# Masking and exponentiating kept attention scores before their transposition, with seven block products in every group

## The chip, the cores and the metric

The kernel runs on one core of one Trainium2 chip, as a single launch. The metric is the device time of that core in microseconds (us); lower is better. A core has five engines that run their own instruction queues in order: TensorE (PE in the profile, with PEld for its weight loads), VectorE (DVE), ScalarE (ACT), GpSimd (POOL) and SyncE (SP), the last two of which mostly issue DMAs here.

## The reference, cut to what matters

Four graph layers on 2708 nodes with 512 features. Only layers 2 and 3 are touched by the change. Layer 2 is a masked softmax whose scores are symmetric before the mask, because queries and keys are the same matrix `h`:

```python
def _L2_gnn_ref(x, adj, weight, bias, node_w, edge_w):
    node_att = softmax(x @ node_w, axis=0)
    h = x @ edge_w
    e = h @ h.T
    e = where(adj > 0, e, -9e15)
    edge_att = softmax(e, axis=1)
    output = adj * (node_att * edge_att) @ (x @ weight)
    return output + bias

def _L3_gnn_ref(x, adj_matrix, spatial_matrix, Wq, bq, ...):
    a = (x @ Wq + bq) @ (x @ Wk + bk).T / sqrt(512)
    a = a + adj_matrix + spatial_matrix        # both are adj
    return softmax(a, axis=-1) @ (x @ Wv + bv)

x = layernorm(x + L2(x, adj));  x = layernorm(x + L3(x, adj, adj))
```

All data is fp32. `adj` itself is not symmetric: `adjT` is a second input with the transposed matrix.

## The kernel before

**Tiles.** The 2708 rows make 22 blocks of 128 (the last has 20 rows) and 11 groups of two blocks. Groups 0 to 9 are full, group 10, the remnant, has 128 + 20 rows. A layer's attention is a walk over pairs (query group gi, key group g): 11 × 11 = 121 steps, the 11 keys of a query group one after the other in the order of `key_order`. A tile of one pair is 128 partitions × 2 × 256: keys on partitions, the group's 256 queries along the row.

**The pipeline of a pair.** `one_score` loads the mask tile with SyncE, forms the scores (sixteen 128x256 matmul records in a full pair, since an fp32 product takes two records) and masks them: ScalarE turns the mask into 0 or −9e15 (L1742), VectorE takes the minimum with the scores out of PSUM into the tile `e` (L1743) and updates a running maximum (L1328). When a group's 11 pairs are scored, `largest` and `spread` make the negated maximum of each query and lay it along the row of every partition (`nmax`). `begin_exp` adds `nmax` (VectorE, L1386) and exponentiates (ScalarE, L1387); `end_exp` adds the tile to the running sum `acc` (VectorE, L1398), loads the mask tile again and multiplies with it (VectorE, L1746), and prepares the differences `T` for the products. `one_sum` multiplies with the values on TensorE (L1444) into the banks `po`, and `end` adds the banks up and queues the group's normalization and projection in `later`. The pair of step t is scored at step t, exponentiated at t − 11 and summed at t − 12 (`LAG = NG + 1`).

**Symmetry.** In layer 2 (`mirror`) the raw scores of a pair with g > gi are copied (`s_raw`) and written to DRAM (`kept`). When the roles turn (g < gi) they are read back with queries on partitions (`s_kept`), transposed by four 128x128 TensorE transposes (L1276) into PSUM, and from there masked as any other pair. There are 55 such turned pairs. In a group's own pair (g = gi) only three of four blocks are computed; the fourth is the transpose of the block that ScalarE copies to `s_own` (L1312, L1314).

**Seven or eight products.** A full pair of 2 × 2 blocks needs eight block products with the value halves, or seven with combined values (`S`, made by `combine`) and the differences `T`, of which VectorE makes four blocks in three operations (L1408). Layer 3 uses seven in every group. Layer 2 uses seven in query groups 0 to 5 and eight from `PLAIN_FROM = 6` on. `combine` overwrites one half of the values, so the original is saved to DRAM (`v2_d`, L1654) and loaded back by GpSimd around group 5 (L1893).

**Order.** A loop over t calls layer 2's step, from step 126 on (`start3 = steps + 5`) layer 3's step, then one item of `later`. The order of instructions on each engine is not the order of the text: the framework's scheduler interleaves them. SyncE's loads stand in one queue; a load waits there until its buffer is free (four mask buffers `a_cols`, two `s_kept`), and what stands behind it waits too.

Of the kernel before, what the change touches and what calls it, by code (L numbers as in the profile page):

```python
# [29 lines left out]
def gnn_stack_kernel(  # L30
# [1157 lines left out]
    v2_d = dram.tile([P, NG - 1, HF], F32, name="v2_d")  # L1188
# [27 lines left out]
    def softmax_layer(  # L1216
        att, psum, later, keys, vals, query, score, weigh, load_rest, finish, mirror, plain_from
# [30 lines left out]
        def load_a(gi, g):  # L1248
            c0, w = GSPAN[gi]
            j0, m = GSPAN[g]  # L1250
            a = att.tile([P, GROUP, GW], F32, tag="a", name="a_cols", bufs=4)
            src = adjT[j0 : j0 + m, c0 : c0 + w]
            if g != REMNANT:
                nc.sync.dma_start(a[:, :, :w], src.rearrange("(b p) i -> p b i", p=P))
                return a
            nc.vector.memset(a[:, 1, :], 0.0)
            nc.sync.dma_start(a[:, 0, :w], src[:P])
            for r in range(0, P, Q):
                nc.sync.dma_start(a[r : r + REST, 1, :w], src[P:])
            return a  # L1260

        def one_score(st, k):
            gi, g = st["gi"], st["order"][k]
            c0, w = GSPAN[gi]
            j0, m = GSPAN[g]
            a = load_a(gi, g)
            ps = psum.tile([P, GROUP, GW], F32, tag="ps_s", name="ps_s")
            e = att.tile([P, GROUP, GW], F32, tag="e", name="e", bufs=LAG + 2)
            sizes = [BLOCKS[it][1] for it in GROUPS[gi]]
            if mirror and g < gi:  # L1270
                s = att.tile([P, GROUP, GW], F32, tag="q", name="s_kept", bufs=2)
                for dst, src in rows_of(gi, s, kept[g, gi]):
                    nc.sync.dma_start(dst, src)
                for jb in range(GROUP):
                    for b, n in enumerate(sizes):
                        nc.tensor.transpose(  # L1276
                            ps[:, jb, b * P : b * P + n],
                            s[:n, b, jb * P : (jb + 1) * P],
                            ident[:n, :n],
                        )  # L1280
            else:
                own = mirror and g == gi
                for jb, jt in enumerate(GROUPS[g]):
                    j = BLOCKS[jt][0]
                    if jt == NT - 1:

                        parts = psum.tile([P, BANK], F32, tag="tp", name="ps_parts")
                        for c in range(C):
                            nc.tensor.matmul(  # L1289
                                parts[c * Q : (c + 1) * Q, :w],  # L1290
                                keys[:, c, j : j + Q],
                                st["q"][:, c, :],
                                start=True,
                                stop=True,
                            )
                        nc.scalar.copy(e[:, 1, :w], parts[:, :w])
                        nc.tensor.matmul(
                            ps[:, 1, :w], quarters, e[:, 1, :w], start=True, stop=True
                        )
                        continue  # L1300
                    i = jb * P if own else 0
                    for c in range(C):
                        nc.tensor.matmul(  # L1303
                            ps[:, jb, i:w],
                            keys[:, c, j : j + P],
                            st["q"][:, c, i:],
                            start=(c == 0),
                            stop=(c == C - 1),
                        )
                    if own and jb == 0 and g != REMNANT:  # L1310
                        s = att.tile([P, GROUP, GW], F32, tag="x", name="s_own", bufs=4)
                        nc.scalar.copy(s[:, 0, :P], ps[:, 0, P:])  # L1312
                    elif own and jb == 1:
                        nc.tensor.transpose(ps[:, 1, :P], s[:, 0, :P], ident)  # L1314
            if mirror and g > gi:
                s = att.tile([P, GROUP, GW], F32, tag="x", name="s_raw", bufs=4)
                nc.scalar.copy(s, ps)
                for dst, src in rows_of(g, s, kept[gi, g]):
                    nc.gpsimd.dma_start(src, dst)
            score(e[:, :, :w], ps[:, :, :w], a[:, :, :w])  # L1320
            st["e"].append(e)
            if k == 1:
                st["mx"] = att.tile([P, GROUP, GW], F32, tag="mx", name="mx", bufs=1)
                nc.vector.tensor_tensor(
                    st["mx"][:, :, :w], st["e"][0][:, :, :w], e[:, :, :w], ALU.max
                )
            elif k > 1:
                in_pairs(g, w, lambda p: nc.vector.tensor_tensor(*p, ALU.max), st["mx"], st["mx"], e)  # L1328

        def in_pairs(g, w, do, *tiles):  # L1330

            if g != REMNANT:
                do([t[:, :, :w] for t in tiles])
            else:
                do([t[:, 0, :w] for t in tiles])
                do([t[:REST, 1, :w] for t in tiles])

        def largest(st):
# [3 lines left out]
            mx = st["mx"]  # L1342
            nc.vector.tensor_tensor(mx[:, 0, :w], mx[:, 0, :w], mx[:, 1, :w], ALU.max)
            tp = psum.tile([P, C, P], F32, tag="tp", name="tp_mx")
            nm = small.tile([P, GROUP], F32, tag="nm", name="nm")
            dg = att.tile([P, GROUP, P], F32, tag="dg", name="dg", bufs=1)
            sizes = [BLOCKS[it][1] for it in GROUPS[gi]]
            for b, n in enumerate(sizes):
                nc.tensor.transpose(tp[:n, b, :], mx[:, 0, b * P : b * P + n], ident)
            runs = [(0, GROUP, P)] if gi != REMNANT else [(b, 1, n) for b, n in enumerate(sizes)]  # L1350
            for b, count, n in runs:
# [4 lines left out]
                nc.vector.tensor_tensor(  # L1356
                    dg[:n, some, :n],
                    ident[:n, :n].unsqueeze(1).to_broadcast([n, count, n]),
                    nm[:n, some].unsqueeze(2).to_broadcast([n, count, n]),
                    ALU.mult,  # L1360
                )
            st["dg"] = dg

        def spread(st):

            gi, dg = st["gi"], st["dg"]
            w = GSPAN[gi][1]
            pb = psum.tile([P, BANK], F32, tag="tp", name="pb")
            if gi != REMNANT:
                nc.tensor.matmul(  # L1370
                    pb[:, :w], ones, dg.rearrange("p b i -> p (b i)"), start=True, stop=True
                )
            else:
                for b, it in enumerate(GROUPS[gi]):
                    n = BLOCKS[it][1]
                    nc.tensor.matmul(
                        pb[:, b * P : b * P + n], ones[:n], dg[:n, b, :n], start=True, stop=True
                    )
            st["nmax"] = att.tile([P, GW], F32, tag="nmax", name="nmax", bufs=2)
            nc.scalar.copy(st["nmax"][:, :w], pb[:, :w])  # L1380

        def begin_exp(st, k):
            w = GSPAN[st["gi"]][1]
            e = st["e"][k][:, :, :w]
            nm = st["nmax"][:, :w].unsqueeze(1).to_broadcast([P, GROUP, w])
            nc.vector.tensor_tensor(e, e, nm, ALU.add)  # L1386
            nc.scalar.activation(e, e, AF.Exp)  # L1387

        def end_exp(st, k):
# [3 lines left out]
            if k == 0:  # L1393
                st["acc"] = att.tile([P, GROUP, GW], F32, tag="acc", name="acc", bufs=1)
                nc.vector.tensor_copy(st["acc"][:, :, :w], e[:, :, :w])
            else:
                acc = st["acc"]
                in_pairs(g, w, lambda p: nc.vector.tensor_tensor(*p, ALU.add), acc, acc, e)  # L1398
            if weigh:
                weigh(e[:, :, :w], load_a(gi, g)[:, :, :w])  # L1400
            if g != REMNANT and gi < plain_from:
# [10 lines left out]
                st.setdefault("t", {})[k] = t  # L1412
# [3 lines left out]
        def row_sums(st):  # L1416
# [4 lines left out]
            nc.vector.tensor_tensor(acc[:, 0, :w], acc[:, 0, :w], acc[:, 1, :w], ALU.add)  # L1421
            pr = psum.tile([P, BANK], F32, tag="tp", name="pr")
            rs = small.tile([P, GROUP], F32, tag="rs", name="rs")
            for b, it in enumerate(GROUPS[gi]):
                n = BLOCKS[it][1]
                nc.tensor.matmul(
# [6 lines left out]
                nc.vector.reciprocal(rs[:n, b : b + 1], pr[:n, b : b + 1])  # L1433
            st["rs"] = rs

        def one_sum(st, k):
# [16 lines left out]
            if gi == REMNANT:  # L1453
                i = [slice(0, P), slice(w - Q, w)]
                if g != REMNANT:
                    v0, v1 = full[:, GROUP * g, :], full[:, GROUP * g + 1, :]
                    terms = [(0, e[:, 0], v0[:, :HF]), (0, e[:, 1], v1[:, :HF])]
                    if gi < plain_from:
                        d = st["t"].pop(k).rearrange("p q i -> p (q i)")
                        terms += [(1, e[:, 0], S[:, g, 0, :]), (1, d, v1[:, HF:])]  # L1460
                    else:
# [517 lines left out]
```

## Time and profile before

| what | value |
|---|---|
| time, median of 3 runs | 3224.51 us (3223.3 to 3234.12) |
| profiled execution, its own time | 3230.21 us |
| its span, first to last instruction | 3228.4 us |
| layer 2's attention, by the trace | from 1617 us to about 2340 us |
| layer 3's attention | from about 2356 us to the end |
| TensorE, VectorE, ScalarE busy over the span | 98%, 66%, 42% |
| granted TensorE clock over the span | 0.995 |

A busy line of the profile gives an engine's busy time and instruction count. A matmul's duration in the trace includes the pipeline's depth and overlaps its neighbours: a 128x256 record has a mean of 386 ns, while records that follow each other without a wait start 216 ns apart. Matmul cost is therefore counted here by the distance between starts, and a wait of TensorE shorter than about 0.15 us cannot be seen in its busy share.

### The profile page before, as it was taken

How to read it: one execution, taken by the hardware profiler on the slowest of the kernel's cores; microseconds unless marked ns; L12 is line 12 of the kernel's file. 1: busy time of each engine (PE TensorE's matmuls, PEld its weight loads, DVE VectorE, ACT ScalarE, POOL GpSimd, SP SyncE). 2: the span in 40 equal slices, each digit the busy share in tenths (PEclk: the TensorE clock that was granted, in tenths of full speed). 3: DMA queues.
4: the chain of work that ended last, by engine and by line, in shares of the span. 5: the costliest groups of instructions: out<-in, count | busy, mean ns of one | idle time of the engine just before them, and what ended most of it. 6: DMA issues, size and time to landing. Idle time of an engine off the chain costs nothing. (4 is left out here: it accounts for less than half of the span.)

```text
span 3228.4 us, 35961 instructions
## 1 busy us (share of the span) xinstructions
PE 3169.6 (98%) x13440; PEld 2144.0 (66%) x13440; DVE 2122.0 (66%) x3654; ACT 1345.5 (42%) x1460; POOL 212.2 (7%) x316
## 2 busy tenths in 40 slices
PE   8999999999999999999999999999999999999999
PEld 5444444444444446875587887777668888888886
DVE  7889987876686685444366677866645555555565
ACT  6898896477867451001133333433311111111111
POOL 1100100000000000001111111211110000000000
PEclk9999999999999999999999999999999999999999
DMA  7867865156455414541154444555441111111110
GB/s 273 309 226 249 291 231 201 45 173 221 172 173 197 156 58 119 143 113 48 54 155 128 134 144 138 169 153 168 121 127 41 49 49 49 49 52 49 49 51 29
DMA packets 209240, 432.42 MB, mean 134 GB/s; under 512 B 22186, under 2 KB 138774, under 8 KB 203242
## 3 DMA queue, kind: packets, MB, share of 16 engines
q1 hardware_dynamic: 184370, 324.15, 32.9%
q0 software_dynamic: 24256, 103.88, 8.8%
q8 instruction: 105, 1.72, 0.2%
q10 hardware_dynamic: 440, 2.10, 0.2%
q14 instruction: 69, 0.57, 0.1%
HBM read 331.38 MB, written 97.21 MB: 133 GB/s over the span
## 5 line engine op out<-in xcount | busy, mean ns | idle before, releaser
L416 DVE SCALAR_TENSOR_TENSOR t<-t,a 128x2708 f32<-128x2708 f32 (+1 forms) x152 | 450.2, 2975 | 144.6 <-ACT t L408 140.5
L1444 PE MATMUL po<-sup,e 128*128 128x256 f32 (+1 forms) x2000 | 497.4, 386 | 8.1 <-DVE e L1746 6.6
L408 ACT ACTIVATE t<-f1b,f2h 128x1354 f32<-128x1354 f32 (+1 forms) x304 | 415.8, 1412 | 46.9 <-PE po L504 36.4
L417 ACT ACTIVATE t<-t 128x2708 f32<-128x2708 f32 (+1 forms) x152 | 373.2, 2456 | 99.7 <-DVE t L416 99.5
L504 PE MATMUL po<-t,xw 128*128 128x452 f32 (+3 forms) x1056 | 410.3, 552 | 4.2 <-ACT t L417 3.6
L1303 PE MATMUL ps_s<-q,hT 128*128 128x256 f32 (+1 forms) x1848 | 405.6, 372 | 0.0
L504 PE MATMUL po<-t,emb 128*128 128x452 f32 (+3 forms) x1056 | 398.9, 546 | 4.0 <-ACT t L417 3.8
L1444 PEld LDWEIGHTS po<-sup,e 128*128 128x128 f32 (+1 forms) x2000 | 348.4, 185 | 77.1 <-issue 22.4
L1303 PEld LDWEIGHTS ps_s<-q,hT 128*128 128x128 f32 x1848 | 340.0, 190 | 50.4 <-issue 6.7
L504 PEld LDWEIGHTS po<-t,xw 128*128 128x128 f32 (+1 forms) x1056 | 189.6, 190 | 213.2 <-issue 196.1
L504 PEld LDWEIGHTS po<-t,emb 128*128 128x128 f32 (+1 forms) x1056 | 194.0, 191 | 202.0 <-issue 191.7
L1832 DVE SCALAR_TENSOR_TENSOR e<-a_cols,ps_s 128x512 f32<-128x512 f32 (+1 forms) x121 | 80.2, 663 | 284.8 <-PE ps_s L1303 249.5
L1444 PE MATMUL po<-held,T 128*128 128x256 f32 x960 | 240.2, 384 | 0.9 <-DVE T L1408 0.8
L1303 PE MATMUL ps_s<-hT 128*128 128x256 f32 (+2 forms) x968 | 215.8, 373 | 8.1 <-ACT s_own L1312 7.5
L1387 ACT ACTIVATE e<-e 128x512 f32<-128x512 f32 (+1 forms) x242 | 143.4, 612 | 147.0 <-DVE e L1386 146.3
L1303 PEld LDWEIGHTS ps_s<-hT 128*128 128x128 f32 x968 | 178.3, 192 | 38.0 <-ACT s_own L1312 10.7
L1742 ACT ACTIVATE a_cols<-a_cols,neg_big 128x512 f32<-128x512 f32 (+1 forms) x121 | 85.1, 704 | 278.5 <-DMA a_cols<-in_adjT_dram 228.3
L1444 PEld LDWEIGHTS po<-held,T 128*128 128x128 f32 x960 | 182.3, 192 | 28.1 <-DVE T L1408 2.7
L1156 PE MATMUL ps_nb<-hid_hi,at 128*128 128x512 f32 x484 | 185.6, 390 | 0.4 <-DVE at L1148 0.4
L1156 PE MATMUL ps_nb<-hid_lo,at 128*128 128x512 f32 x462 | 180.1, 390 | 0.0
L1386 DVE TENSOR_TENSOR e<-e,nmax 128x512 f32<-128x512 f32 (+1 forms) x242 | 154.6, 666 | 18.0 <-ACT nmax L1380 16.8
L1824 ACT ACTIVATE q<-ps_wide,uq 128x256 f32<-128x256 f32 (+1 forms) x44 | 20.5, 466 | 326.7 <-PE ps_wide L1207 326.7
(267 smaller groups left out, 3906.1 us busy)
## 6 DMA issues: line engine op xcount, KB each, us to landing
a_cols<-in_adjT_dram SPq DMA_DIRECT2D x300, 256.0 KB
a<-adj_d SPq DMA_DIRECT2D x108, 677.0 KB
a<-in_adjT_dram SPq DMA_DIRECT2D x42, 677.0 KB
adj_d<-a POOLq DMA_DIRECT2D x42, 677.0 KB, 5.1
kept<-t POOLq DMA_DIRECT2D x20, 1354.0 KB, 6.6
t<-kept SPq DMA_DIRECT2D x20, 1354.0 KB
raw<-in_adjT_dram SPq DMA_DIRECT2D x105, 256.0 KB
scores<-s_raw POOLq DMA_DIRECT2D x45, 256.0 KB, 3.0
```

The lines of the kernel that those rows point to most:

```text
L408: tanh = nc.scalar.activation(tv[:, k, :], f1b[k][:n, :w], AF.Tanh, bias=f2h[:n, jt, h : h + 1], scale=0.5,)
L416: step = nc.vector.scalar_tensor_tensor(tv, tv, GUARD, ab, ALU.add, ALU.mult)
L417: exp = nc.scalar.activation(tv, tv, AF.Exp, scale=0.5)
L504: nc.tensor.matmul(po[HB * k + q][:, :qw], values[r : r + n, jt, h * P : (h + 1) * P], t[r : r + n, k, q0 : q0 + qw], start=(place == 0), ...
L1156: nc.tensor.matmul(pos[it][:n], at, half[:, jt, :], start=(jt == 0 and k == 0), stop=(jt == NT - 1),)
L1303: nc.tensor.matmul(ps[:, jb, i:w], keys[:, c, j : j + P], st["q"][:, c, i:], start=(c == 0), stop=(c == C - 1),)
L1386: nc.vector.tensor_tensor(e, e, nm, ALU.add)
L1387: nc.scalar.activation(e, e, AF.Exp)
L1444: nc.tensor.matmul(po[bank][rows, half, :], lhsT, rhs, start=(k == 0 and half == 0) if first is None else first, stop=last, skip_group_che ...
L1742: nc.scalar.activation(a, a, AF.Identity, bias=neg_big[: a.shape[0]], scale=1.0e30)
L1824: lambda o, ps: nc.scalar.activation(q[:, o, :w], ps, AF.Identity, bias=uq[:, o : o + 1]),
L1832: nc.vector.scalar_tensor_tensor(e, a, 2.0, ps, ALU.mult, ALU.add)
```

## The change

In layer 2 a turned pair is no longer transposed before it is masked. The kept scores are loaded straight into the tile `e`, with queries on partitions, beside a tile of `adj` itself (not `adjT`); masking and running maximum take place in that layout (`score_rows`). The maximum of the turned pairs is a reduction along the row (`largest`). `begin_exp` exponentiates with the maximum as ScalarE's per-partition bias, one instruction for each of the two blocks, and takes the row sums with the same instructions (`accum_out`); the addition of `nmax` and the addition to `acc` fall away for these pairs. In `end_exp` four transposes bring the exponentiated tile to PSUM, and the multiplication with the mask reads it from there. `row_sums` adds the two kinds of sums.

Every group of both layers now uses seven products; `PLAIN_FROM`, `v2_d` and its loads are gone. Score masks have buffers of their own in layer 2 (three `a_score`), the four `a_cols` hold the weights alone, and each load is put into the program a step before its use (`fetch`, `fetch_weights`). `begin_exp` stands a step further ahead of the sum: `LAG = NG + 2`, `start3 = steps + 6`, `e` has `lag + 3` buffers. In own and remnant pairs the part that waits for a ScalarE copy (`rest`) stands behind the step's products. `spread` uses the maximum as a broadcast weight against the identity instead of a diagonal matrix.

```diff
@@ begin_exp, end_exp
         def begin_exp(st, k):
-            w = GSPAN[st["gi"]][1]
-            e = st["e"][k][:, :, :w]
-            nm = st["nmax"][:, :w].unsqueeze(1).to_broadcast([P, GROUP, w])
-            nc.vector.tensor_tensor(e, e, nm, ALU.add)
-            nc.scalar.activation(e, e, AF.Exp)
+            gi, g = st["gi"], st["order"][k]
+            w = GSPAN[gi][1]
+            if not turned(gi, g):
+                e = st["e"][k][:, :, :w]
+                nm = st["nmax"][:, :w].unsqueeze(1).to_broadcast([P, GROUP, w])
+                nc.vector.tensor_tensor(e, e, nm, ALU.add)
+                nc.scalar.activation(e, e, AF.Exp)
+                return
+            m = st["count"][0]
+            st["count"][0] += 1
...
+            for b, it in enumerate(GROUPS[gi]):
+                n = BLOCKS[it][1]
+                e = st["e"][k][:n, b, :]
+                nc.scalar.activation(
+                    e, e, AF.Exp, bias=st["nm"][:n, b : b + 1],
+                    accum_out=st["sums"][:n, b, m : m + 1],
+                )
...
+            if turned(gi, g):
+                ps = psum.tile([P, GROUP, GW], F32, tag="ps_s", name="ps_e")
+                for jb in range(GROUP):
+                    for b, it in enumerate(GROUPS[gi]):
+                        n = BLOCKS[it][1]
+                        nc.tensor.transpose(
+                            ps[:, jb, b * P : b * P + n],
+                            e[:n, b, jb * P : (jb + 1) * P],
+                            ident[:n, :n],
+                        )
+                weigh(e[:, :, :w], ps[:, :, :w], st["wa"].pop(k)[:, :, :w])
...
-            if g != REMNANT and gi < plain_from:
+            if g != REMNANT:
                 t = att.tile([P, 2 * GROUP, P], F32, tag="T", name="T", bufs=2)
@@ new: fetch, fetch_weights, score_rows
+        def fetch(t):
...
+            e = att.tile([P, GROUP, GW], F32, tag="e", name="e", bufs=lag + 3)
+            st["e"].append(e)
+            a = tile_a()
+            st["a"].append(a)
+            if not turned(gi, g):
+                load_a(a, gi, g)
+                return
+            i0, w = GSPAN[gi]
+            j0 = GSPAN[g][0]
+            for dst, src in rows_of(gi, a, adj[i0 : i0 + w, j0 : j0 + GW]):
+                nc.sync.dma_start(dst, src)
+            for dst, src in rows_of(gi, e, kept[g, gi]):
+                nc.sync.dma_start(dst, src)
+        def fetch_weights(t):
+            gi, k = divmod(t, NG)
+            a = att.tile([P, GROUP, GW], F32, tag="a", name="a_cols", bufs=4)
+            states[gi]["wa"][k] = load_a(a, gi, states[gi]["order"][k])
+        def score_rows(st, k):
+            gi, e, a = st["gi"], st["e"][k], st["a"][k]
+            for x, y in by_rows(gi, e, a):
+                score(x, x, y)
+            running_max(st, k, "rows")
@@ one_sum
-            if gi >= plain_from:
-                for jb, jt in enumerate(GROUPS[g]):
-                    if jt != NT - 1:
-                        for b, i in enumerate((i1, i2)):
-                            for h in range(2):
-                                product(
-                                    2 * b + h,
...
@@ the step
+            if 0 <= t + AHEAD < total:
+                fetch(t + AHEAD)
+            if weigh and 0 <= t + AHEAD + 1 - lag < total:
+                fetch_weights(t + AHEAD + 1 - lag)
+            front = t + 2 - lag
...
@@ the main loop
-    LAG = NG + 1
-    PLAIN_FROM = 6
+    AHEAD = 1
+    LAG = NG + 2
...
-        start3 = steps + 5
+        start3 = steps + 6
```

## The prediction, made before the changed kernel was run

> **What bounds the kernel now.** I read the page's busy shares first, then the stretches of layer 2 one group at a time (from one group's maximum to the next), then TensorE's waits there, then the chain of waits for the cost of one product.
>
> ```profile
> PE 3169.6 (98%) x13440; PEld 2144.0 (66%) x13440; DVE 2122.0 (66%) x3654; ACT 1345.5 (42%) x1460; POOL 212.2 (7%) x316
> ```
>
> TensorE is the bound of the whole. The stretches, with length, busy time by engine, TensorE's clock, DMA share and GB/s:
>
> ```profile
> core 0: us, PE busy (x) PEld busy (x) DVE busy (x) ACT busy (x) POOL busy (x), PEclk, DMA share, GB/s
> 2003.20:2069.20 66.00, 63.33 (x296) 50.02 (x295) 52.37 (x115) 24.19 (x39) 12.84 (x19) 0.97 0.56 163
> 2069.20:2139.20 70.00, 65.43 (x303) 52.46 (x301) 44.00 (x84) 24.98 (x40) 9.40 (x12) 0.95 0.50 148
> 2139.20:2201.00 61.80, 59.43 (x293) 47.98 (x292) 41.44 (x78) 21.16 (x35) 8.97 (x9) 1.00 0.54 159
> 2201.00:2262.10 61.10, 58.59 (x281) 46.39 (x280) 41.77 (x79) 22.71 (x36) 12.03 (x8) 0.97 0.58 172
> 2262.10:2322.90 60.80, 57.60 (x268) 43.44 (x267) 37.03 (x80) 19.08 (x32) 5.71 (x6) 1.00 0.42 116
> 2577.60:2655.90 78.30, 78.30 (x376) 67.83 (x375) 43.75 (x101) 12.67 (x22) 1.08 (x2) 1.00 0.18 50
> ```
>
> The last row is a group of layer 3: no visible idle time. The four before it sum groups 6 to 9, those with eight products. Counting each matmul record by the distance at which its kind follows itself (216 ns for 256 columns, 109 for a transpose), layer 2 from 1617.0 to 2322.9 holds 643 us of matmul work in 705.9 us, so 63 us of waiting; those four stretches hold 221 in 253.7, so 32. A layer-3 group holds 76.5 in 78.3. TensorE's longest waits between 1600 and 2360 (total, times, longest):
>
> ```profile
> PE ps_s L1303 <- ACT s_own L1312: 7.5, 3, 3.1
> PE po L1444 <- DVE e L1746: 6.6, 6, 2.3
> PE ps_s L1297 <- ACT e L1296: 5.4, 3, 3.2
> ```
>
> And the chain of waits (start, duration, records) prices a pair's sum: 16 records are eight products, 14 are seven.
>
> ```profile
> 2104.63 4.91 PE po L1444 x14
> ...
> 2175.21 3.02 PE po L1444 x14
> 2178.67 3.46 PE po L1444 x16
> ```
>
> **Products.** Groups 6 to 9 have ten full pairs each: 40 pairs lose one product. One product is 2 × 216 ns = 0.43 us (3.46 − 3.02 agrees): 40 × 0.43 = **−17.3 us**. The remnant query group and the remnant key have as many products as before. Nothing else stands beside these on TensorE, so this comes off the path unless the differences `T` are late.
>
> **VectorE, which must make T.** Rows of 2069 to 2323, then the two T forms of layer 2:
>
> ```profile
> L1746 DVE TENSOR_TENSOR e<-e,a_cols 128x512 f32<-128x512 f32 x44 | 32.5, 740 | 29.8 <-DMA a_cols<-in_adjT_dram 29.8
> L1386 DVE TENSOR_TENSOR e<-e,nmax 128x512 f32<-128x512 f32 x44 | 31.2, 719 | 4.8 <-ACT nmax L1380 4.8
> L1398 DVE TENSOR_TENSOR acc<-acc,e 128x512 f32<-128x512 f32 x36 | 25.5, 707 | 0.9 <-ACT e L1387 0.5
> ...
> L1408 DVE TENSOR_TENSOR T<-e,T 128x128 f32<-128x128 f32 x120 | 35.4, 299 | 1.9
> L1408 DVE TENSOR_TENSOR T<-e 128x256 f32<-128x256 f32 x60 | 26.3, 438 | 7.3 <-PE po L1444 5.7 <-DMA v_d<-v 1.3
> ```
>
> A turned pair loses L1386 and L1398. Neighbours overlap by some 0.08 us, so they free about 1.28 us, in all 55 × 1.28 = 70 us. In groups 6 to 9 that is 30 pairs, 38 us. Against it come 40 × (0.44 + 2 × 0.30) = 42 us of T, about 10 us of bank additions in `end` and 2 us of row reductions. VectorE there goes from 44.0 + 41.4 + 41.8 + 37.0 = 164 us to about 180, TensorE's work from 221 to 204. A step that is turned on both sides costs TensorE 3.02 + 4 × 0.11 = 3.46 us and VectorE multiply 0.68, T 1.04, mask 0.64, maximum 0.64 = 3.0 us: it fits, with little room. In groups 0 to 5 VectorE only loses work. The multiplication now reads PSUM and the mask SBUF: the row that reads PSUM (L1743) has 0.68, the one that reads SBUF 0.74, so between −0.06 and +0.06 us a pair; I take 0.
>
> **ScalarE.** One exponential (0.63 us) becomes two of 256 with a bias per partition. L1742 has such a bias: 0.721 us at 512 elements, 0.536 at 296, so 0.50 at 256 and 1.0 for two. Writing the sums is not in the trace: at least 0, at most about 0.2 each (a 128x1 ACTIVATE, L108, has 0.20). That is 0.4 to 0.8 more a pair, 20 to 44 us in all, on an engine with 35 to 40 us idle in each of these stretches. It is hidden by the step between an exponential and its transposes (3.5 us). Behind a late one would stand, on TensorE, the step's scores and sum; bounds 0 and 2 us a group, 22 us; I take it near 0, inside the last term below.
>
> **Loads.** Bytes per pair stay the same: mask, kept scores, weights. Only `v2_d` goes (ten stores, ten loads, hidden in GpSimd's queue). SyncE's queue still has one head, but masks and weights no longer share four buffers, and scores need no transposition before their buffer is free. VectorE waited 29.8 us for weights in the last four groups; most of that goes. On TensorE it shows as the wait for L1746, 6.6 us: **−4**, the rest stays because VectorE is fuller. Past the moved loads SyncE must wait for `e` buffers, but the sum that frees one lies three steps back.
>
> **Own and remnant pairs.** In the trace `s_own` was late because its copy stood behind a mask (L1742) that waited for its DMA. Now products stand between the copy and the transpose, and the mask arrives earlier: **−7.5**. The wait for L1296 goes the same way: −3 of 5.4 in layer 2 (the one before layer 3 has no products to hide behind) and 0.3 us in each of layer 3's 11 groups: **−6** together. What is late next is VectorE's T.
>
> **The clock.** Two stretches around two waits of 2.5 to 3.3 us:
>
> ```profile
> 2101.48:2108.30 6.82, 5.96 (x19) 5.16 (x20) 3.10 (x7) 1.53 (x4) 0.54 (x1) 0.50 0.41 119
> ...
> 2171.00:2174.50 3.50, 1.21 (x8) 0.78 (x8) 1.60 (x4) 0.87 (x2) 0.00 (x0) 1.00 0.57 172
> ```
>
> After the first the clock was 0.50 for 6.8 us, and a sum took 4.91 instead of 3.02. Layer 2 has four such stretches, 17.1 us, so 8.5 us lost, behind waits of 2.1, 2.5, 3.3 and 2.2 us; a wait of 2.5 us (the second row) cost nothing. The Trainium skill (TensorE: Matmul & The Clock Gate, § Why this matters for your kernels) says that only idle gaps above some 3 us bring the clock down. By that rule three of the four would not have happened, and ending these waits would be worth at most 3.4 us of clock; by the rows it is 8.5. I take the rows, and that new waits bring some back: **−5**.
>
> **New waits.** T has two buffers, and the projection's output (`v3`) takes one until its store lands (3.2 us in the trace, behind GpSimd's 2 us addition). In groups 6 to 9 nothing needed T before. Bounds: 0, or 18 us as in the slower rival. The nearest row is 2003 to 2069, where T was made and VectorE had 52 us against 58 of matmul work: 7.6 us of waiting, 1.7 of it clock, against 3 in easy groups. I take 1.5 a group for four, **+6**. The longer lag and `start3` move both ends by a step without adding work: 0, bounds −3 and +3. Two 128-wide products instead of one 256-wide in `spread` cost the same.
>
> **Sum.** −17.3 − 4 − 7.5 − 6 − 5 + 6 = −33.8. The profiled execution took 3230.2, so 3196.4; the median of the runs shown lies 5.7 lower (3224.5), and I give the time against it: **3191 us**, own range 3178 to 3204.
>
> **Rivals.**
> - *The waits only move.* Products are saved, but ended waits come back as waits for T: 3224.5 − 17.3 = 3207, to 3215. For it: VectorE at 180 of 204. Against: the waits for s_own and for loads have causes that the change takes away. 0.24.
> - *Layer 2 runs as smoothly as layer 3.* Waiting falls from 63 to some 3 a group, 30, and layer 3's 3 us go: −17.3 − 33 − 3 = −53, 3171 (3155 to 3178). Against: the tight last groups. 0.14.
> - *VectorE becomes the bound (slower).* In those four stretches it reached 164 / 253.7 = 0.65 of the time. If chains through PSUM, ScalarE and two T buffers let it do no better, 180 us take 277: +23, and with 8 regained in earlier groups about 3240. It decides from a share of 0.71 (180 / 253.7) downward. Against it: 0.79 was reached in 2003 to 2069 with T. 0.06.
> - *No change in effect*: late T eats just the 17 us: about 3222. 0.06.
>
> **Numbers.** Forecast 0.50. Within 0.3% (9.7 us) is what a measurement of this kernel can't tell from no change. Faster is 0.50 + 0.24 + 0.14 = 0.88, same 0.06, slower 0.06. The range 3164 to 3213 takes in the forecast, nearly all of the first rival and most of the second.
>
> **What would show it.** TensorE's records of 40 products gone, and layer 2's four late stretches near 215 us instead of 253.7; no wait for s_own; fewer stretches at clock 0.50; VectorE's wait for a_cols below 10 us there; layer-3 groups at 78.0. It would be wrong if TensorE's waits in those groups name T or the multiplication for more than 10 us, or the transposes of `e` wait for ScalarE.

## The result, and the profile after

| | before | after |
|---|---|---|
| median of 4 runs each, same chip | 3225.46 us (3223.3 to 3234.12) | 3197.54 us (3193.31 to 3200.05) |
| ratio, with its 95% interval | | 0.9907 [0.9885, 0.9929] |
| profiled execution, its own time / its span | 3230.21 / 3228.4 us | 3195.56 / 3193.5 us |

The ratio is worth 30 us (23 to 37), the difference of the medians 28. The profiled executions differ by 34.65 us, more than that, because the one of before lay 5.7 us above its median; the forecast for that difference was 33.8, and for the time 3191 us. Of the page, the busy line first, then layer 2 in stretches from one group's maximum to the next, the columns as in the prediction.

```profile
PE 3145.5 (98%) x13400; PEld 2125.6 (67%) x13400; DVE 2102.4 (66%) x3746; ACT 1356.7 (42%) x1623; POOL 202.7 (6%) x296
```

TensorE has 40 records fewer: 80 records of 40 products are gone, and `spread` now makes two narrower products of each one (40 records more). VectorE is less busy although it makes 120 more operations for `T`.

```profile
2054.60:2114.30 59.70, 58.03 (x279) 45.76 (x278) 43.57 (x106) 24.44 (x55) 9.27 (x10) 1.00 0.53 161
2114.30:2170.90 56.60, 55.57 (x271) 43.53 (x270) 43.46 (x105) 22.07 (x55) 8.85 (x9) 1.00 0.59 172
2170.90:2226.30 55.40, 52.26 (x258) 40.56 (x257) 41.55 (x103) 26.00 (x62) 5.74 (x8) 1.00 0.61 183
2226.30:2276.70 50.40, 49.49 (x245) 38.47 (x244) 40.68 (x120) 23.43 (x66) 6.14 (x6) 1.00 0.47 135
2539.90:2618.20 78.30, 78.30 (x378) 67.83 (x377) 43.46 (x101) 12.87 (x22) 1.07 (x2) 1.00 0.18 51
```

The four late groups, those that went from eight products to seven (the first four rows), sum 222.1 us, where they took 253.7. VectorE's part of them is 43.57 + 43.46 + 41.55 + 40.68 = 169.3 us, or 0.76 of the time. A layer-3 group (last row) takes what it took. Counted by the distance between starts, the four hold 201 us of matmul work and 21 of waiting (before: 221 and 32).

TensorE's waits between 1600 and 2360 us (total, times, longest):

```profile
PE po L1546 <- DVE T L1503: 4.8, 7, 1.4
PE ps_s L1342 <- DVE e L1832: 3.4, 1, 3.4
```

The waits for `s_own` (7.5), for the multiplication with the mask before a sum (6.6) and for the remnant's copy (5.4) no longer lead the list. The new first row is the one the prediction charged for, `T`. VectorE's waits from 1600 to 2277 us:

```profile
...
DVE T L1503 <- DMA v_d<-v: 22.1, 7, 6.6
DVE e L1832 <- PE ps_e L1475: 13.7, 11, 2.4
...
DVE e L1832 <- DMA a_cols<-in_adjT_dram: 8.5, 6, 3.9
```

VectorE's wait for the weights' DMA was 77.1 us in 49 places before (1617 to 2323 us); it is 8.5 us. In its place the longest wait for a DMA is one that the forecast named but did not price by itself: a buffer of `T` that still holds the projection's output `v3`, until GpSimd's store of it (`v_d<-v`) has landed. The longest wait of all, 72.2 us for ScalarE's copies of raw scores (39.2 before), cost TensorE little: its waits for the masking (L1829) sum 0.2 us.

**Where the 34.65 us came from.** From layer 2's start to its last maximum, 705.9 us became 659.7 (−46.2): matmul work −28.0, waiting 63.1 to 44.9 (−18.2). From there to the second maximum of layer 3, 177.0 became 185.4 (+8.4: work +5.5, waiting +2.9), and the tail of the program 43.0 became 45.8 (+2.8, nearly all work). About 9 us of the work that left the first stretch comes back in the other two: the longer lag moved sums past these ends and removed and added none. Together the work is some 19 us less and the waiting some 16.

### The profile page after: what moved, and what is told of

Its sections match the earlier page's. It is cut to its first block, busy times and chain, and to the rows that moved or that the text cites. A ratio compares the mean times of both kernels' runs of the same rounds, so it can differ in the third digit from the quotient of the medians.

```text
span 3193.5 us, 36039 instructions
## 1 busy us (share of the span) xinstructions
PE 3145.5 (98%) x13400; PEld 2125.6 (67%) x13400; DVE 2102.4 (66%) x3746; ACT 1356.7 (42%) x1623; POOL 202.7 (6%) x296
## 4 chain that ended last, share of the span: by engine, by line
PE 85%; DVE 6%; issue 3%; ACT 3%; DMA 2%; POOL 0%; SPq 0%; DVEq 0%; ACTq 0%; POOLq 0%
PE po L504 22%; PE po L1546 18%; PE ps_s L1342 17%; PE ps_nb L1156 7%; PE ps_wide L1206 5%; PE psm L541 3%; PE ps_sup L1734 2%; PE ps_mlp L792 2%; PE ps_hid L128 2%; PE ps_dec L923 2%; PE ps_v L128 1%; DVE t L416 1%; ACT t L408 1%; ACT t L417 1%; DVE e L1832 1%
## 5 line engine op out<-in xcount | busy, mean ns | idle before, releaser
L1546 PE MATMUL po<-sup,e 128*128 128x256 f32 (+1 forms) x1512 | 396.9, 384 | 3.1 <-DVE c L1627 2.1
L1546 PEld LDWEIGHTS po<-sup,e 128*128 128x128 f32 (+1 forms) x1512 | 264.2, 185 | 59.3 <-issue 21.5
L1546 PE MATMUL po<-held,T 128*128 128x256 f32 x1200 | 294.8, 380 | 4.8 <-DVE T L1503 4.8
L1546 PEld LDWEIGHTS po<-held,T 128*128 128x128 f32 x1200 | 226.3, 190 | 38.9 <-DVE T L1503 7.6
L1828 ACT ACTIVATE a_score<-a_score,neg_big 128x512 f32<-128x512 f32 (+2 forms) x131 | 88.9, 686 | 256.6 <-DMA a_score<-in_adjT_dram 108.1
L1452 ACT ACTIVATE e<-e 128x512 f32<-128x512 f32 (+1 forms) x187 | 113.6, 617 | 133.2 <-DVE e L1451 130.1
L1503 DVE TENSOR_TENSOR T<-e 128x256 f32<-128x256 f32 x200 | 84.2, 421 | 120.2 <-PE po L1546 97.1
```

What stands on the lines that cost most here:

```text
L1546: nc.tensor.matmul(po[bank][rows, half, :], lhsT, rhs, start=(k == 0 and half == 0) if first is None else first, stop=last, skip_group_che ...
L1828: nc.scalar.activation(a, a, AF.Identity, bias=neg_big[: a.shape[0]], scale=1.0e30)
```

## Experiments

Ratios are to the kernel before on the same chip; the chips differ between some of the rows. The changed kernel itself was run again among them (`a_again`): 0.9918 [0.9905, 0.9932], median 3197.65 us. Several of the differences between rows below are near the width of an interval, and this is said where it bears on the argument.

| kernel | what it is | median us | ratio |
|---|---|---|---|
| `b_seven` | before, seven products in all groups | 3225.22 | 0.9998 [0.999, 1.0006] |
| `b_rest` | before, last part of own and remnant pairs behind the sum | 3211.14 | 0.996 [0.9947, 0.9972] |
| `b_restseven` | both of these | 3219.49 | 0.9976 [0.9967, 0.9985] |
| `b_five` | before, five mask buffers | 3221.4 | 0.9992 [0.9984, 1.0001] |
| `a_eight` | after, eight products from group 6 | 3204.59 | 0.9941 [0.9927, 0.9954] |
| `a_inline` | after, own and remnant parts in their old place | 3203.77 | 0.9929 [0.9917, 0.9942] |
| `a_noahead` | after, loads in the step that uses them | 3188.28 | 0.989 [0.9874, 0.9905] |
| `a_dvetwice` | after, row maximum taken twice | 3201.17 | 0.9933 [0.992, 0.9945] |
| `a_v3c` | after, `v3` not in a buffer of `T` | 3184.88 | 0.9876 [0.9862, 0.989] |
| `a_v3c_again` | the same once more | 3188.49 | 0.9877 [0.9862, 0.9892] |
| `a_v3c0` | `a_v3c` and `a_noahead` together | 3185.24 | 0.9869 [0.9855, 0.9882] |

### The products: alone, and taken back

`b_seven` gives the old kernel the seven products and nothing else; `a_eight` takes them from the new one.

```diff
@@ b_seven, from before
-    v2_d = dram.tile([P, NG - 1, HF], F32, name="v2_d")
-                    nc.gpsimd.dma_start(v2_d[:, it // GROUP, :], sup[:, it, HF:])
-    PLAIN_FROM = 6
+    PLAIN_FROM = NG
-                nc.gpsimd.dma_start(sup[:, GROUP * g, HF:], v2_d[:, g, :])
@@ a_eight, from after
+    PLAIN_FROM = 6
+    v2_d = dram.tile([P, NG - 1, HF], F32, name="v2_d")
-            if g != REMNANT:
+            if g != REMNANT and gi < plain_from:
                 t = att.tile([P, 2 * GROUP, P], F32, tag="T", name="T", bufs=2)
...
+            if gi >= plain_from:
+                for jb, jt in enumerate(GROUPS[g]):
...
```

`a_eight` has the stores and loads of `v2_d` and the eight-product branches of `one_sum` and `end` back as they stood before.

> The kernel before with seven products in every group of layer 2 and nothing else changed. My theory: without the two operations that row-wise masking takes from VectorE, VectorE has 164 + 42 + 10 = 216 us of work beside 204 of TensorE in the last four groups, so VectorE is the bound there and the 17 us of products come back as waits for T: between 10 us faster and 10 us slower than before, 3215 to 3235. Rival: T would have fitted anyway, and this gains the full 17 us, 3206 to 3210.

> The changed kernel with eight products in groups 6 to 10 of layer 2 again (and the original value halves saved and loaded back), all else as changed. My theory: the 40 products are worth 17.3 us of TensorE and the T that they need costs at most the 6 us of waits for T and the bank additions, so this is 11 to 17 us slower than the changed kernel, about 3211. Rival (the waits only move): the products were paid for by waits for T, so this stays within 5 us of the changed kernel, 3197 to 3202.

In the old kernel 40 fewer products are worth nothing: 0.9998. The first of its late groups, as a stretch:

```profile
2063.20:2127.70 64.50, 60.40 (x284) 47.89 (x283) 50.97 (x114) 24.28 (x39) 8.71 (x10) 0.97 0.52 153
```

and TensorE's waits in its layer 2:

```profile
PE po L1443 <- DVE e L1743: 12.9, 8, 2.3
PE ps_s L1302 <- ACT s_own L1311: 5.6, 3, 2.2
PE po L1443 <- DVE T L1407: 2.4, 3, 1.6
```

VectorE has 51 us of work in this stretch of 64.5 us, where the changed kernel's has 43.6 in 59.7. The four late groups take 244.2 us, 9.5 less than before though 17.3 us of products are gone, and the sums wait for the masked weights (L1743, 12.9 us where it was 6.6) more than for `T` itself: the differences stand ahead of the next pair's multiplication on VectorE. So waits took back about half of the work in these stretches. The traces do not show the whole loss, for they are not of median executions: the profiled one of `b_seven` took 3221.57 us, 3.7 under its median, and 8.6 less than the profiled one of before. The median granted clock of the 13 executions was 0.995, and 0.996 for before; a thousandth is about 3 us, so time at half clock is a part of what the median lost.

In the changed kernel the products are worth 0.9941 against 0.9907 and 0.9918, that is 0.0023 to 0.0034 of 3225 us, 7 to 11 us. I had expected 11 to 17; it is at the lower edge of that or below, and above the rival's 5. The intervals overlap a little (0.9927 is the lower end of one, 0.9929 and 0.9932 are the upper ends of the others), so the size is less sure than the sign.

### The last part of own and remnant pairs

```diff
@@ b_rest, from before: one_score
-                    elif own and jb == 1:
-                        nc.tensor.transpose(ps[:, 1, :P], s[:, 0, :P], ident)
...
+            def rest():
+                if mirror and g == gi and g != REMNANT:
+                    nc.tensor.transpose(ps[:, 1, :P], held[:, 0, :P], ident)
+                elif g == REMNANT and not (mirror and g < gi):
+                    nc.tensor.matmul(ps[:, 1, :w], quarters, e[:, 1, :w], ...)
...
+            if (g == gi and mirror) or g == REMNANT:
+                return rest
@@ b_rest: the step, behind sum_step
+            if rest:
+                rest()
@@ a_inline, from after: one_score
                 nc.scalar.copy(held[:, 0, :P], ps[:, 0, P:])
+                block(1, P)
...
-            if own or g == REMNANT:
-                return rest
             rest()
```

In an own pair `b_rest` also computes its two key blocks in the opposite order, as the changed kernel does, so that the block to be copied comes last.

> The kernel before with only the order of own and remnant pairs changed: the part that waits for ScalarE's copy stands behind the step's sum. My theory, as in the prediction: the waits for s_own (7.5 us) and for the copy of the remnant parts (3 us of layer 2) go, with some of the half clock behind them: 8 to 14 us faster than before, 3213 to 3219. Rival: the copy was late because a mask's load was late, and without the earlier loads the same wait moves to the next instruction: within 4 us of before.

> The kernel before with the later place of the own and remnant pairs' last part and with seven products in every group of layer 2; kept scores are still transposed before they are masked. My theory: VectorE has about 216 us beside 204 of TensorE in the last four groups, so the products come back as waits for T and for the multiplication, as in the order of before: within 4 us of the later place alone (ratio 0.996). Rival: in the mended order T fits, and the ratio is about 0.991, as with the whole change.

> The changed kernel with the last part of own and remnant pairs in its old place, right behind the copies of ScalarE. My theory: the waits for s_own and for the copy of the remnant parts come back with some half clock: 6 to 13 us slower than the changed kernel, ratio 0.994 to 0.996. Rival: with the loads a step ahead ScalarE is not held by a mask any more, the copies are in time, and this is within 3 us of the changed kernel, ratio 0.991.

Alone this part takes 12.7 us off the kernel before, the largest single piece. TensorE's waits in layer 2 of `b_rest` have no row for `s_own`:

```profile
PE po L1455 <- DVE e L1759: 6.7, 7, 2.3
PE po L1455 <- DVE c L1554: 4.4, 3, 1.5
PE po L1455 <- DVE T L1419: 2.7, 2, 1.5
```

and no stretch of layer 2 has the clock at 0.50 in this execution; the only one between 1600 and 3200 us lies behind it, at 2403 us. (Its mean clock, 0.999, is the highest of the five; the others have 0.997 or 0.998.) Adding the seven products to it (`b_restseven`) costs about 5 us: 0.9976 against 0.996, the intervals meeting at 0.9967 to 0.9972. The same rows there:

```profile
PE po L1454 <- DVE e L1756: 13.0, 9, 2.3
PE po L1454 <- DVE c L1553: 5.9, 6, 1.5
PE po L1454 <- DVE T L1418: 4.4, 4, 1.8
```

All three grow, all three are VectorE's: 13.8 us become 23.3. So the order of own pairs is not what the products lack in `b_seven`. It must be in what is left of the change: masking by rows, the separate buffers, the longer lag, the new `spread`. No run takes these apart. On top of `b_rest` with eight products that rest is worth about 6 us (`a_eight` 0.9941 against 0.996, intervals overlapping); with seven it is worth some 19 to 22 (0.9976 against 0.9918 and 0.9907).

In the changed kernel the old place of the last part costs 3.5 to 7 us (`a_inline`), at or below the lower edge of the 6 to 13 of my theory and above the rival's 3; the intervals overlap, so it may be less. Three of its executions took 3200.7 to 3201.2 us with a granted clock of 0.998, three 3206.3 to 3207.8 with 0.996: the clock alone moves one kernel by as much as this part is worth. TensorE then waits 1.2 us for `s_own` and 1.8 for the remnant's copy, where it was 7.5 and 5.4: something else in the change makes these copies less late. It is not that ScalarE waits less for its masks (222 us over layer 2, where it was 228), and what it is stays open. The parts of the change don't seem to be additive.

### The loads

```diff
@@ b_five, from before
-            a = att.tile([P, GROUP, GW], F32, tag="a", name="a_cols", bufs=4)
+            a = att.tile([P, GROUP, GW], F32, tag="a", name="a_cols", bufs=5)
@@ a_noahead, from after
-    AHEAD = 1
+    AHEAD = 0
```

> The kernel before with five mask buffers instead of four. My theory: VectorE's waits for weights (75 us over layer 2) come from masks and weights sharing four buffers, so one more takes half of them away; TensorE's waits for the multiplication and for s_own shrink: 5 to 12 us faster than before. Rival: loads are late for the order in SyncE's queue, not for buffers: within 4 us of before.

> The changed kernel with each load put into the program in the step of its use instead of a step before (AHEAD = 0). My theory: what ends the waits for loads is that score masks and weights no longer share four buffers and that a mask's buffer is freed without a transposition; the scheduler places the loads by free buffers, so this is within 4 us of the changed kernel. Rival: the step ahead is what counts, and VectorE's waits for a_cols, a_score and kept scores come back: 8 to 20 us slower, 3206 to 3218.

Neither of my expectations held in its numbers. A fifth shared mask buffer gives 0.9992 [0.9984, 1.0001], not the 5 to 12 us I gave it; VectorE still waits 24.1 us for `a_cols` in the late groups (29.8 before). And the step ahead is not what the gain needs, as my theory of `a_noahead` had it: without it the kernel is as fast or, beyond the 4 us I allowed, faster, 0.989 against 0.9907 and 0.9918. VectorE's waits in its layer 2 show why it can be faster:

```profile
...
DVE e L1832 <- DMA a_cols<-in_adjT_dram: 11.5, 7, 6.6
...
DVE T L1503 <- DMA v_d<-v: 10.0, 4, 3.4
```

The weights are 3 us later than in the changed kernel, the wait for `v3`'s store is 12 us shorter. The scheduler orders the other instructions anew with it, so this run moved more than the loads.

What ended VectorE's 77 us of waits for the weights' masks is therefore only half settled: not the number of shared buffers, not the step ahead. What remains is that weights and score masks no longer share buffers, or that a turned pair's buffer no longer waits for a transposition; neither was taken back alone. Nor do these waits cost TensorE much as long as VectorE has room: in `b_rest` they are longer than before (85.8 us over layer 2, 40.2 in its late groups), and there TensorE waits 1.4 us for the multiplication.

### How much room VectorE has

```diff
@@ a_dvetwice, from after: score_rows
             running_max(st, k, "rows")
+            if len(st["mx"]["rows"]) == 2:
+                running_max(st, k, "rows")
```

> The changed kernel with the running maximum of the turned pairs taken twice (same result), 45 operations of 128x512 and some of the remnant more, about 0.62 us each on VectorE: some 19 us in the four stretches that sum groups 6 to 9 and 9 us before. My theory: VectorE has about 169 us of work beside 201 of TensorE there, so a part hides: 3 to 9 us slower than the changed kernel. Rival (VectorE is all but the bound in those stretches): 15 to 25 us slower. Second rival (VectorE does not matter): within 2 us.

The slower rival of the prediction needs VectorE to be full at a share of 0.71 or lower (180 us in 253.7). Here the four late groups hold 188.9 us of VectorE work in 225.4 us, a share of 0.84, and cost 3.3 us more than the changed kernel's. The whole kernel is 3.5 to 5 us slower by its medians and by the ratio to `a_again` on the same chip (0.9933 against 0.9918, 3201.17 against 3197.65), for 26 us of added VectorE work (2128.0 us on its page, 2101.9 for `a_again`), 20 of them in the late groups. The intervals overlap, so all that can be said is that it is a few microseconds at most. VectorE is near enough for a part of added work to count, by the medians one microsecond in five to seven, and it is not the bound.

It also limits what `b_seven` shows. There VectorE's share was 200.5 / 244.2 = 0.82, no higher than here, and yet all of the gain was lost. The two differ in the loads: in the late groups VectorE waits 14.0 us for the weights in `b_seven` and 12.8 in `b_restseven`, and not at all here. Late masks without the added work stand in `b_rest`: VectorE's share of the late groups was 163.4 / 237.6 = 0.69, with 40.2 us of such waits, and they cost TensorE no more than the 1.4 us named above. Added work without late masks is this run, a few us. In the old kernel with seven products both come together. That the two together take the 17 us is read from these traces; the kernels differ in more than these two, and no run changed the masks alone.

### The buffer that `v3` takes

In the changed kernel the longest wait of TensorE in layer 2 stands at 1757 us. Its timeline (start, duration, engine, line; in brackets the idle time before it and what ended it):

```profile
1754.30 0.54 POOL L1875 DMA_DIRECT2D v_d<-v  x1 [4.89 <-ACT e L1368]
...
1759.47 0.43 DVE L1503 TENSOR_TENSOR T<-e 128x256 f32<-128x256 f32 x1 [3.60 <-DMA v_d<-v]
...
1760.46 0.68 DVE L1832 TENSOR_TENSOR e<-ps_e,a_cols 128x512 f32<-128x512 f32 x1
...
1761.20 6.55 PE L1342 MATMUL ps_s<-hT 128*128 128x256 f32 x16 [3.39 <-DVE e L1832]
```

GpSimd issues the store of `v3` at 1754.3. VectorE stands for 3.60 us before `T`, whose next buffer `v3` holds. Behind `T` on VectorE stands the multiplication that frees the transposes' PSUM bank, and for that bank TensorE waits 3.39 us. Then the clock is at half: 16 records take 6.55 us instead of 16 × 0.216 = 3.46. This cost is one chain: 3.4 + 3.1 us in this one place. It is no accident of one execution: the other five traces with `v3` in that place (`a_again`, `a_eight`, `a_inline`, `a_noahead`, `a_dvetwice`) have a wait of 2.1 to 3.6 us within 6 us of it, each beside a wait of `T` for the same store (2.6 to 3.8 us) and with half clock behind it; the three traces without `v3` there have none.

```diff
@@ a_v3c, from after (a_v3c0 has AHEAD = 0 as well)
-                v = att.tile([P, F], F32, tag="T", name="v3", bufs=2)
+                v = att.tile([P, GROUP, F], F32, tag="c", name="v3", bufs=1)[:, 0, :]
```

> The changed kernel with the projection's output v3 in the tile c (free by then) instead of one of the two T buffers. My theory: T waited 12 us for v3's stores, and one such wait led to TensorE's 3.4 us wait for the multiplication at 1761 us and the half clock of 6.8 us behind it; both go: 5 to 9 us faster than the changed kernel, about 3190. Rival: T is late for other reasons as well and the next wait takes the place: within 2 us of the changed kernel.

> The changed kernel with v3 in the tile c and each load in the program in the step of its use (AHEAD = 0). Both alone were faster than the changed kernel. If they are independent: ratio 0.985 to 0.986. If both only removed the same waits of TensorE around 1761 us: as v3 in c alone, 0.9876.

> The changed kernel with v3 in the tile c, once more, to stand beside the others on one chip. All theories: ratio to before 0.987 to 0.989.

> The changed kernel unaltered, so that it stands beside the experiments on one chip. All theories: ratio to before 0.990 to 0.992, about 3196.

With `v3` in the tile of the bank sums (`c`), the wait is gone from VectorE's list, and TensorE's longest between 1600 and 2400 us are two single ones:

```profile
PE tp_mx L1418 <- DVE mx L1398: 2.0, 1, 2.0
PE ps_e L1475 <- DVE e L1829: 1.6, 1, 1.6
```

No stretch of layer 2 has the clock at 0.50, and the group that holds the wait took 72.5 us instead of 78.7. TensorE's row for `T` (4.8 us) is gone as well; with the chain of 6.5 us this is about the gain. In all it is 9 to 13 us faster than the changed kernel by the medians, the upper edge of the 5 to 9 I expected or above it: 0.9876 and 0.9877 against 0.9907 and 0.9918, which makes it the best of all kernels here with `a_v3c0`, 1.2 to 1.3% faster than before. `a_v3c0` adds nothing that can be told apart (0.9869 [0.9855, 0.9882]). That fits `a_noahead`, which had already lost half of the same wait: the two gains are, at least in part, one.

## Why the prediction was right, step by step

It was right in its mechanism: the products go, VectorE has room for `T`, the waits for ScalarE's copies end, and some new waits come. The time of 3197.5 us lies in the likeliest case's own range, between the forecast and its slower neighbour. That the profiles differ by 34.65 us where the sum had 33.8 is in part luck: by medians it is 28, by the ratio 30, the term for layer 3 came to nothing, and the one for the clock hangs on which executions were profiled.

- **Products, −17.3.** The matmul work fell by 19 us by count, so the term stands. Its worth net of the waits it brings is 7 to 11 us by `a_eight`; the sum had −17.3 + 6 = −11.3, the upper end of that.
- **VectorE has room for `T`.** This was the condition of the forecast, and `b_seven` and `b_restseven` show that the products alone are worth nothing: without the masking by rows and what comes with it they give 0 and +5 us. But it is not the share of VectorE alone: at 0.84 with early masks (`a_dvetwice`) most of the gain stayed. The size was off to the safe side, 169 us against 180. `T` cost 41 us as priced; the freed operations came to 43 us against 38 (the three groups of 32.5, 31.2 and 25.5 us became 29.1, 9.5 and 7.8, so that the multiplication fell too), and the bank additions to 6 instead of 10.
- **`s_own` −7.5, copies −3, clock −5.** The rows are gone, that of the copies with all of its 5.4 us, and `b_rest` gives these three terms by themselves: 12.7 against 15.5 less the part of the clock that belongs to other waits. In layer 2 and behind it the time at half clock fell from 17.1 to 6.8 us, 5.1 us of gain, and to 10.2 in the trace of `a_again`, 3.4 us. The rule of the Trainium skill that idle gaps should stay under some 3 us (TensorE: Matmul & The Clock Gate, § Why this matters for your kernels) would have allowed 3.4 at most. The total doesn't tell the two apart, then; the rows do, for three of the four stretches of before stand behind waits of less than 3 us, and the last section shows what decided.
- **Copies in layer 3, −3: mis-sized, it is 0.** A layer-3 group took 78.3 us before and after. The 0.3 us were read as a wait for ScalarE's copy (L1296). In both traces they stand behind the last 32-column record of the remnant's scores (L1289 before, L1361 after), and the record that follows it 0.309 us later is a product of the sum in both, which needs no copy: the scheduler had already put the products there before. The same 0.309 us stand behind it where scores follow (at 1640 us before), so the gap is the 32-column record's and not the copy's.
- **Loads, −4.** TensorE's row for L1746 (6.6 us, 1.4 of them in the late groups) is down to below 1 where it stands before a sum; the 3.4 us for the same operation (L1832) are the chain behind `v3` above. VectorE's wait for `a_cols` in the late groups is 0.4 us. The reason given was separate buffers and no transposition before release, and only its alternatives were tested (`b_five`, `a_noahead`).
- **New waits, +6, and the lag at 0.** In the late groups, for which the term was made, TensorE's waits for `T` (3.9 us), the multiplication (0.9) and the bank sums `c` (1.1) come to 5.9. What the prediction missed lies outside them. It did name `v3`'s hold on a buffer of `T`, but priced it only in groups 6 to 9, where nothing needed `T` before; it bit hardest at 1757 us, in an earlier group that had made `T` all along, with 6.5 us, and moving it saves 9 to 13 us. The longer lag gave back 2.9 us of waiting between the layers, at the edge of its −3 to +3. The late groups took 222 us where the list of signs had 215, but 215 is less than the sum itself gives: its terms that lie in them (−17.3 for products, −7.5, −3 for the copy, 1 of the 4 for loads, the clock's share, +6) make about 226 to 228.
- **ScalarE.** Two exponentials, each with the reading of its accumulator, rows of 1660 to 2277 us:

```profile
...
L1461 ACT ACTIVATE e<-e,nm 128x256 f32<-128x256 f32 x90 | 44.6, 497 | 6.0 <-DVE nm L1425 6.0
...
L1461 ACT ACTIVATION_READ_ACCUMULATOR e<-e,nm 128x1 f32 x90 | 16.9, 188 | 0.0
```

A turned pair costs 2 × (0.497 + 0.188) = 1.37 us, inside the 1.0 to 1.4 of the prediction and near its upper end, and hidden: TensorE waited 0.4 us in all for these exponentials. (ScalarE's idle time in the stretches of before was 38 to 45 us by the rows, not 35 to 40.)

The rival of no change in effect (what is late eats the 17 us) describes the old kernel with seven products, and not this one; the change also takes work and late masks off VectorE, how much each of the two counts was not taken apart. The smooth layer 2 (3171) fell short because 45 us of waiting stay in layer 2 where it had 30; the `v3` buffer explains about ten.

## What to carry to other kernels

An operation saved on the bound engine counts only as far as the engine that prepares its operands has room and gets its own inputs in time: price both, stage by stage, and make the room first (here the same 40 products were worth 0, +5 and −7 to −11 us in three surroundings). A short step that waits for another engine's copy goes behind independent work of its own engine; it took 12.7 us off here and needed no other part of the change. When an operation uses a ring of buffers, look at who else lives in that ring: an unrelated tile that holds a buffer until its DMA lands can hold up all that stands behind it, 9 to 13 us here.

## What the runs showed of the hardware that was not expected

- Reading the accumulator is an instruction of its own, 0.188 us for each exponential that also sums, about as long as the 128x1 operation of L108 (0.202 us).
- VectorE's multiplication took the same from PSUM as from SBUF, 0.680 and 0.675 us. Rows of 2054 to 2277 us of the changed kernel:

```profile
...
L1832 DVE TENSOR_TENSOR e<-ps_e,a_cols 128x512 f32<-128x512 f32 x29 | 19.7, 680 | 9.4 <-PE ps_e L1475 7.8 <-ACT nmax L1443 1.5
...
L1832 DVE TENSOR_TENSOR e<-e,a_cols 128x512 f32<-128x512 f32 x14 | 9.4, 675 | 0.5 <-DMA a_cols<-in_adjT_dram 0.4
```

- The clock falls to half for 3.4 or 6.8 us, never another length in layer 2 of these traces. In the profile of before it did so behind waits of 2.1, 2.2, 2.5 and 3.3 us, and not behind two others of 2.5 and 3.4 us (at 2174 and 2298 us; all counted by starts, which is 0.17 us more than the idle time that a view shows): the length of a wait alone doesn't tell. What tells is where it falls. In each of the 14 traces all falls stand a multiple of 3.413 us apart; the four in layer 2 of before, at 1951.29, 2016.15, 2101.48 and 2248.25 us, are 19, 25 and 43 such windows from one to the next. Windows on this grid, the first two just ahead of a fall, the last two around the wait of 3.4 us that cost nothing:

```profile
1947.88:1951.29 3.41, 1.46 (x8) 1.12 (x7) 3.41 (x10) 0.20 (x1) 0.00 (x0) 1.00 0.48 159
2244.84:2248.25 3.41, 1.38 (x7) 0.90 (x6) 1.29 (x2) 0.87 (x2) 0.00 (x0) 1.00 0.68 189
2292.63:2296.04 3.41, 1.88 (x16) 1.04 (x14) 1.72 (x3) 0.64 (x2) 0.00 (x0) 1.00 0.21 55
2296.04:2299.45 3.41, 1.74 (x9) 1.59 (x10) 0.99 (x3) 0.71 (x2) 0.00 (x0) 1.00 0.09 28
```

  TensorE was idle for 1.95 and 2.03 us in the first two, and for 1.53 and 1.67 us in the others, because the end of a window cuts the longer wait in half. From 1600 to 2460 us of all 14 traces, 30 windows at full clock are followed by half clock, with 1.66 us of idle time or more, and no window without a fall has more than 1.85. So idle time of about half a window was enough, and a longer wait that lay across the end of a window could cost nothing. The free-running activity window of about 3.4 us that the Trainium skill describes (TensorE: Matmul & The Clock Gate, § What's actually happening) agrees with this grid.
